# Expert outputs summed per token in DRAM by accumulating indirect transfers, in place of gathers at the end

## The chip, the core and the metric

The kernel runs as one program on one core of a Trainium2 chip. Its engines are TensorE (PE, whose weight loads are listed as PEld), VectorE (DVE), ScalarE (ACT) and GpSimd (POOL); SyncE (SP) issues most of the transfers, and POOL issues the indirect ones, whose rows are named by a list of indices in SBUF. The metric is the device time of one execution in microseconds; the time of a kernel is the median over its runs.

## The reference

The input x has 4 rows of 1024 tokens of 128 numbers. Two layers follow, each with two branches that read the same normalized x and are added to it:

```python
x = L0_attn_x
xn = _layernorm(x, axis=-1)
x = x + _L0_attn_ref(xn, ...) + _L0_ffn_ref(xn, ...)
xn = _layernorm(x, axis=-1)
x = x + _L1_attn_ref(xn, ...) + _L1_ffn_ref(xn, ...)
```

The first layer is an attention of 16 heads with one shared key and value head, and a SwitchHead attention: 8 heads with 8 experts each for values and outputs, of which gates choose two. The second is a FAVOR+ attention (16 heads, 64 random features; exponentials of queries and keys, sums over the tokens, no attention matrix) and a mixture of experts. The change is in the mixture:

```python
logits = xf @ gate_w + gate_b                    # 4096 tokens, 8 experts
top_w, top_i = jax.lax.top_k(logits, 2)
gw = jax.nn.softmax(top_w, axis=-1)
combine = (gw[:, :, None] * jax.nn.one_hot(top_i, E)).sum(axis=1)
for e in range(E):                               # 128 -> 512 -> 128
    h = jax.nn.gelu(xf @ w1[e] + b1[e], approximate=False)
    out = out + combine[:, e:e + 1] * (h @ w2[e] + b2[e])
shared = jax.nn.gelu(xf @ ws1 + bs1) @ ws2 + bs2
return (out + shared).reshape(orig_shape)
```

So only two of the eight experts count for a token, each with its share.

## The kernel before

**Layer 0** goes over the four rows b and, in each, over the heads; it lasts to about 3015 us of the span. TensorE's order of instructions is written out by hand; VectorE, ScalarE and POOL are ordered by the scheduler of the tile framework. In it, as soon as x of a row is whole, layer 1's normalization and its **router** run for that row (L222 to L280), scattered between heads of the next row. The router takes the two best experts per token (oh0, oh1), counts with two matmuls how many tokens of each expert came before, and so gives every (token, expert) pair a slot: expert e owns rows 4096e to 4096e + 4095 of the DRAM tensor `sorted_x`. `share` holds the two softmax weights. Then the row's normalized tokens are written there: for each of 8 tiles of 128 tokens VectorE makes `xslot` (L270, two buffers), and POOL issues two indirect scatters of it (L274), one per chosen expert. Each waits for the one before to land, as both write `sorted_x`. Before all that, behind row 0's first attention, `sorted_x` is filled with zeros by one SP transfer from a small zero tile (L535 to L542), since the last block of an expert is only partly used.

**Layer 1** has its order written by hand for TensorE and SP. Two things run in turn.

The attention of row b has two generators: `favor_keys` (19 steps) and `favor_queries` (20 steps). They run in five stages: keys of row 0; then queries of row 0 with keys of row 1; 1 with 2; 2 with 3; queries of row 3. These are 19, 39, 39, 39 and 20 steps. `project` (L957 to L969) starts each: qT or kT, and its square on POOL (L968), which `dg` (L1024) needs.

The filler is the rest of the mixture: `shared` (17 steps: the shared feed-forward) and then `experts` (L1288 on), 39 blocks of 256 rows with two half steps each, 78 half blocks. 39 is enough for every way in which the tokens can be divided over the experts; which expert a block has, and where it starts in `sorted_x`, is worked out by VectorE before (tile `block`, read by SP with value loads). A block j goes through `load` (SP: its rows xg from `sorted_x`, w1, w2; three buffers each), `turn` (two transposes on TensorE, L1306), `one` (8 matmuls pb, L1316, with gelu on ScalarE, L1322) and `two` (8 matmuls pe, L1331; a VectorE copy yb of the result, L1336; a store to the DRAM tensor `sorted_y`, L1337). Iteration j of the loop does load(j), turn(j-1), one(j-2), two(j-3), and gives way after `one` and after `two`.

The stages set how much filler goes beside each attention step, by a rate; with a rate of 1.0 in all stages the 95 filler steps are used up at the end of stage 2:

```python
for _ in run(*its):
    due += rate
    while due >= 1.0:
        due -= 1.0
        next(filler, None)
```

At the end `combine` (L1353 to L1367) fetches both expert rows of each token back: per tile of 128 tokens and per chosen expert one indirect gather on POOL from `sorted_y` (L1359; the row numbers are worked out from the slots, L940 to L953) and one VectorE multiply-add of it, by the share, into x (L1365). After four tiles SP writes the output's 256 KB (L1401). There are 64 gathers, 64 multiply-adds, 8 outputs; each gather waits for one of six y buffers.

Each engine works through its own queue in order, so an instruction that waits holds up all behind it there.

Of the kernel before, what the change touches and what calls it, by code (L numbers as in the profile page):

```python
# [9 lines left out]
F32 = mybir.dt.float32  # L10
I32 = mybir.dt.int32
BF16 = mybir.dt.bfloat16
AF = mybir.ActivationFunctionType
ALU = mybir.AluOpType
# [40 lines left out]
PER = SLOTS // MB  # L55

# [8 lines left out]
def two_layers(ctx: ExitStack, tc: tile.TileContext, a: dict, out: bass.AP):  # L65
# [84 lines left out]
    slot = fixed([P, 2, B, NT], "slot")  # L150
# [11 lines left out]
    sorted_x = hbm.tile([ME * SLOTS, D], F32, tag="sorted_x", name="sorted_x")  # L162
    sorted_y = hbm.tile([NBLK * MB, D], F32, tag="sorted_y", name="sorted_y")
# [58 lines left out]
    def router(b):  # L222
# [25 lines left out]
        for n in range(NT):  # L248
            nc.vector.tensor_tensor(mask[:, n, :], pcv[:, 0, n, :], filled, ALU.add)
            nc.vector.tensor_tensor(filled, pcv[:, 1, n, :], filled, ALU.add)  # L250
        for k, oh in enumerate((oh0, oh1)):
            to = rt.tile([P, NT, ME], F32, tag="to", name=f"to{b}_{k}")
            nc.vector.tensor_tensor(to, oh, mask, ALU.mult)
            nc.vector.tensor_reduce(slot[:, k, b, :], to, axis=AX.X, op=ALU.add)
        at_slot = rt.tile([P, 2, NT], I32, tag="at_slot", name=f"at_slot{b}")
        nc.vector.tensor_copy(at_slot, slot[:, :, b, :])
# [11 lines left out]
        for n in range(NT):  # L268
            xn = rt.tile([P, D], F32, tag="xslot", name=f"xslot{b}_{n}", bufs=2)
            nc.vector.tensor_scalar(  # L270
                xn, x[b][:, n, :], mv[:, n, 0:1], rstd[:, n : n + 1], ALU.subtract, ALU.mult
            )
            for k in range(2):
                nc.gpsimd.indirect_dma_start(  # L274
# [8 lines left out]
    with ExitStack() as l0:  # L283
# [219 lines left out]
        def mqa_out(b):  # L503
# [28 lines left out]
            if b == 0:  # L532
                nc.sync.dma_start(gw, a["gate_w"])
                nc.sync.dma_start(gb, a["gate_b"].unsqueeze(0).to_broadcast([P, ME]))
                empty = sw.tile([P, SE, P], F32, tag="gs", name="empty", bufs=3)  # L535
                nc.gpsimd.memset(empty, 0.0)
                flat = empty.rearrange("p e d -> p (e d)")
                n = ME * SLOTS * D // (P * SE * P)
                nc.sync.dma_start(
                    sorted_x.rearrange("(p n k) d -> p n (k d)", p=P, n=n),  # L540
                    flat.unsqueeze(1).to_broadcast([P, n, SE * P]),
# [355 lines left out]
    for e in range(1, ME):  # L897
# [4 lines left out]

    past = brief(0, NBLK, ME - 1, "past")
    full = [P, NBLK, ME - 1]
    nc.vector.tensor_tensor(
        past, bcast(num[:, 0:NBLK], ME - 1),
        upto[:, 0 : ME - 1].unsqueeze(1).to_broadcast(full), ALU.is_ge,
# [3 lines left out]
    nc.vector.tensor_tensor(  # L911
        past, past, nb[:, 0 : ME - 1].unsqueeze(1).to_broadcast(full), ALU.mult
    )
    nc.vector.tensor_reduce(of[:, 1, :], past, axis=AX.X, op=ALU.add)
    nc.vector.tensor_tensor(of[:, 1, :], num[:, 0:NBLK], of[:, 1, :], ALU.subtract)
    nc.vector.tensor_scalar(of[:, 1, :], of[:, 1, :], float(PER - 1), None, ALU.min)
    nc.vector.scalar_tensor_tensor(
        of[:, 1, :], of[:, 0, :], float(PER), of[:, 1, :], ALU.mult, ALU.add
    )
    block = fw.tile([P, 2, NBLK], I32, tag="block", name="block")  # L920
# [15 lines left out]

# [528 lines left out]
```

## Time and profile before

| | us |
|---|---|
| runs shown | 3592.8, 3598.83, 3599.55 |
| median | 3598.83 |
| profiled execution, its own time | 3601.22 |
| its span | 3599.4 |
| layer 1: stages 0 to 4 start at about | 3040, 3173, 3303, 3425, 3519 |
| last matmul ends at | 3568 |
| TensorE busy in the span | 3356.3 |

The mean granted clock of TensorE is 0.962 of full speed. In the profile a line such as `L1331 PE MATMUL pe<-w,hb` is a group of instructions: source line, engine, operation, what it writes and reads. "Busy" is the time in which an engine executes, "idle before" the time in which it stood still just before that instruction, with what ended that. Registers, semaphores and the issuing of transfers by SP are not counted as busy. In a table by stretches each engine has its busy time and, in brackets, its instructions; then come the granted clock, the share of time in which the 16 transfer engines were busy, and the rate.

### The profile page before, as it was taken

Reading aid. Unit: us, or ns where it says so; the run is one execution under the profiler, and the core shown is the slowest. Engines: PE = TensorE matmul, PEld = TensorE weight load, DVE = VectorE, ACT = ScalarE, POOL = GpSimd, SP = SyncE. Lnnn points to the kernel's source line nnn. Section 1 sums busy time; section 2 is a strip of 40 time slices with the busy share of each in tenths; the row PEclk is TensorE's granted clock in tenths of the full one; section 3 lists DMA queues with packets and bytes.
Section 4 is the critical chain, followed back from the end, with each engine's and each line's share of the span. In section 5 each row is a group of like instructions: output and inputs, shape, how many; then the busy total and the mean of one; then the engine's idle time right before and its main releaser. Section 6 shows DMA issues by size and latency. Waiting matters only on the chain.

```text
span 3599.4 us, 40579 instructions
## 1 busy us (share of the span) xinstructions
PE 3356.3 (93%) x14270; PEld 1682.1 (47%) x14270; DVE 2506.2 (70%) x4571; ACT 1613.6 (45%) x2800; POOL 1592.9 (44%) x2032
## 2 busy tenths in 40 slices
PE   6999999999999998999999989999999998999973
PEld 3444444444444443444444434444444443478852
DVE  6876678777777778777777687677777765355575
ACT  2344444444444443444445434444444454455521
POOL 3644445444454465444454554444644433100024
PEclk8999999999999998999999999999999998899976
DMA  3000000000410000000000000000000000024302
GB/s 84 19 14 14 21 14 28 7 19 12 180 50 19 12 20 20 19 12 19 14 23 12 17 23 12 19 19 14 27 15 13 6 1 14 31 76 140 104 19 55
DMA packets 146543, 111.46 MB, mean 31 GB/s; under 512 B 11482, under 2 KB 128740, under 8 KB 146340
## 3 DMA queue, kind: packets, MB, share of 16 engines
q1 hardware_dynamic: 142116, 100.46, 9.7%
q0 software_dynamic: 4096, 8.40, 0.8%
q8 instruction: 113, 1.85, 0.2%
q14 instruction: 90, 0.74, 0.1%
q10 hardware_dynamic: 128, 0.02, 0.0%
HBM read 77.12 MB, written 31.33 MB: 30 GB/s over the span
## 4 chain that ended last, share of the span: by engine, by line
PE 77%; DVE 14%; POOL 3%; issue 2%; DMA 2%; ACT 1%; SPq 1%; another core or an unknown queue 0%; POOLq 0%; DVEq 0%; ACTq 0%
PE cp L681 12%; PE ss L649 11%; PE po L702 11%; PE pv L632 11%; PE ov L460 6%; PE sT L470 5%; PE pTp L669 5%; PE mx L416 5%; DVE nmh L422 2%; DVE nms L654 2%; PE qks L613 1%; PE pb L1316 1%; PE pe L1331 1%; DMA sorted_x<-xslot,at_slot 1%; DVE mk L1051 1%
## 5 line engine op out<-in xcount | busy, mean ns | idle before, releaser
L422 DVE TENSOR_REDUCE nmh<-mx 128x1 f32<-128x512 f32 x1024 | 657.4, 680 | 353.6 <-PE mx L416 353.1
L621 POOL TENSOR_TENSOR g_o<-g_o 128x512 f32<-128x512 f32 x256 | 324.9, 1269 | 1224.4 <-DVE g_o L706 1002.4
L477 ACT ACTIVATE pT<-sT 128x512 f32<-128x512 f32 x1024 | 556.3, 601 | 408.0 <-PE sT L470 403.9
L632 PE MATMUL pv<-vw,xnT 128*128 128x512 f32 x1024 | 486.9, 609 | 18.3 <-DVE nmh L422 9.1
L681 PE MATMUL cp<-pTs,vs 128*128 128x512 f32 x1024 | 463.2, 606 | 39.6 <-DVE pTs L673 32.4
L649 PE MATMUL ss<-xnT,qTs 128*128 128x512 f32 x1024 | 492.2, 602 | 6.7 <-DVE gv L636 3.8
L702 PE MATMUL po<-ow,cTs 128*128 128x512 f32 x1024 | 471.8, 593 | 2.5 <-ACT ps L652 2.5
L652 ACT COPY ps<-ss 128x512 f32<-128x512 f32 x512 | 298.6, 587 | 351.7 <-PE ss L649 332.0
L654 DVE TENSOR_REDUCE nms<-ps 128x1 f32<-128x1024 f32 x256 | 310.6, 1213 | 188.7 <-ACT ps L652 188.1
L656 ACT ACTIVATE ps<-ps,nms 128x1024 f32<-128x1024 f32 x256 | 294.2, 1149 | 180.4 <-DVE nms L654 179.4
L636 DVE TENSOR_TENSOR gv<-pv,gates 128x512 f32<-128x512 f32 x512 | 334.7, 681 | 32.2 <-POOL x L712 12.4
L621 POOL TENSOR_TENSOR gv<-gv 128x512 f32<-128x512 f32 x256 | 328.6, 1284 | 34.4 <-DVE gv L636 34.1
L706 DVE TENSOR_TENSOR g_o<-po,go 128x512 f32<-128x512 f32 x512 | 328.4, 680 | 19.1 <-PE po L702 14.2
L681 PEld LDWEIGHTS cp<-pTs,vs 128*128 128x128 f32 x1024 | 193.9, 193 | 287.5 <-issue 231.7
L416 PE MATMUL mx<-ks,qs 72*128 72x512 bf16 x1024 | 310.0, 380 | 11.8 <-DVE nmh L422 5.2
L470 PE MATMUL sT<-qs,ks 75*128 75x512 bf16 x1024 | 308.2, 382 | 11.4 <-DVE ob L499 3.7
L632 PEld LDWEIGHTS pv<-vw,xnT 128*128 128x128 f32 x1024 | 196.0, 194 | 243.8 <-issue 153.9
L649 PEld LDWEIGHTS ss<-xnT,qTs 128*128 128x128 f32 x1024 | 190.9, 191 | 195.4 <-issue 122.7
L669 PE MATMUL pTp<-ident,ps 128*128 128x128 f32 x2048 | 270.1, 275 | 11.6 <-ACT ps L656 9.1
L669 PEld LDWEIGHTS pTp<-ident,ps 128*128 128x128 f32 x2048 | 239.8, 141 | 81.9 <-issue 20.4
L702 PEld LDWEIGHTS po<-ow,cTs 128*128 128x128 f32 x1024 | 179.6, 190 | 157.5 <-issue 136.4
L460 PE MATMUL ov<-pT,va 128*32 128x512 f32 x2048 | 248.5, 601 | 0.0
(269 smaller groups left out, 3901.2 us busy)
## 6 DMA issues: line engine op xcount, KB each, us to landing
w<-in_w_dram SPq DMA_DIRECT2D x78, 256.0 KB
vw<-in_v_w_dram SPq DMA_DIRECT2D x32, 512.0 KB
ow<-in_o_w_dram SPq DMA_DIRECT2D x32, 512.0 KB
sorted_x<-empty SPq DMA_DIRECT2D x1, 16384.0 KB
qs<-qd SPq DMA_DIRECT2D x144, 64.0 KB
xg<-sorted_x SPq DMA_DIRECT2D x39, 128.0 KB
sorted_y<-yb SPq DMA_DIRECT2D x39, 128.0 KB
qd<-qp SPq DMA_DIRECT2D x12, 256.0 KB
```

The source lines that it names most:

```text
L416: nc.tensor.matmul(sc, lhsT=qs[0:NPAIR, i, ts(n, P)], rhs=ks[0:NPAIR, ts(kc, 512)], start=True, stop=True,)
L422: nc.vector.tensor_reduce(halves[:, i, n, kc : kc + 1], sc, axis=AX.X, op=ALU.max)
L460: nc.tensor.matmul(ov[32 * i : 32 * i + 32, :], lhsT=va[:, kt, :], rhs=pT, start=(kt == 0), stop=(kt == NT - 1),)
L470: nc.tensor.matmul(sc, lhsT=ks[:, ts(kt, P)], rhs=qs[:, i, ts(c, 512)], start=True, stop=True,)
L477: nc.scalar.activation(pT, sc, AF.Exp)
L621: nc.gpsimd.tensor_tensor(g[:, 0:4, :], g[:, 0:4, :], g[:, 4:8, :], ALU.add)
L632: nc.tensor.matmul(pv, lhsT=xnT[b][:, ts(n, P)], rhs=unit[u, "w"][0][:, ts(c, 512)], start=True, stop=True,)
L649: nc.tensor.matmul(sc, lhsT=qT[:, ts(n, P)], rhs=xnT[b][:, ts(c, 512)], start=True, stop=True)
L654: nc.vector.tensor_reduce(nm, p, axis=AX.X, op=ALU.max, negate=True)
L669: nc.tensor.transpose(pt[:, ts(k, P)], p[:, ts(4 * k4 + k, P)], ident)
L681: nc.tensor.matmul(cp, lhsT=v[:, kt, :], rhs=pT[:, kt, :], start=(kt == 0), stop=(kt == NT - 1),)
L702: nc.tensor.matmul(po, lhsT=cT[:, ts(qt, P)], rhs=unit[u, "w"][1][:, ts(c, 512)], start=True, stop=True,)
```

## The change

The gathers go, and each block adds its weighted rows to its tokens' sums itself.

- A row of `sorted_x` gets two more numbers (ROW = 130): the token's number, as 32-bit integer, and its share. The router makes one `xslot` per scatter (16 instead of 8 per row of x, still two buffers), and POOL writes the two columns with small copies.
- Rows of `sorted_x` that no token fills hold "nobody": zeros, and the token number 4096, which is a row of the sums that nobody reads. 256 such rows are put behind the last expert, and blocks past the end of the work read these.
- Two DRAM tensors `sums[0]`, `sums[1]` (4224 x 128 each) are filled with zeros ahead of `sorted_x`. The fill of `sorted_x` is by rows of 520 bytes.
- `two` multiplies each half of its result by the share column of xg (two VectorE instructions in place of one copy) and POOL adds it to `sums[q]` at the rows that xg's token column names, by an indirect transfer that accumulates. `sorted_y` and its store go, so do the row numbers. xg has four buffers, and is held until those transfers have read its indices.
- At the end SP reads each chunk of 512 tokens of both sums (16 reads of 256 KB, into the three buffers of w1), VectorE adds them to x (16 adds of 128x512), SP writes the 8 outputs.
- The rates become 0.84, 0.45, 0.45, 0.45, 1.2, so that half blocks go beside the steps of all stages; the few left follow stage 4.
- The squares of L968 move from POOL to VectorE; the zeros of va1 are written once instead of per row.

```diff
+ROW = D + 2
...
+    sorted_x = hbm.tile([ME * SLOTS + MB, ROW], F32, tag="sorted_x", name="sorted_x")
+    sums = [hbm.tile([B * T + P, D], F32, tag=f"sum{q}", name=f"sum{q}") for q in range(2)]
+    token = const.tile([P, B * NT + 1], I32, tag="token", name="token")
+    nc.gpsimd.iota(token, pattern=[[P, B * NT + 1]], base=0, channel_multiplier=1)
...
         for n in range(NT):
-            xn = rt.tile([P, D], F32, tag="xslot", name=f"xslot{b}_{n}", bufs=2)
-            nc.vector.tensor_scalar(
-                xn, x[b][:, n, :], mv[:, n, 0:1], rstd[:, n : n + 1], ALU.subtract, ALU.mult
-            )
             for k in range(2):
+                xn = rt.tile([P, ROW], F32, tag="xslot", name=f"xslot{b}_{n}_{k}", bufs=2)
+                nc.vector.tensor_scalar(
+                    xn[:, 0:D], x[b][:, n, :], mv[:, n, 0:1], rstd[:, n : n + 1],
+                    ALU.subtract, ALU.mult,
+                )
+                i = b * NT + n
+                nc.gpsimd.tensor_copy(xn[:, D : D + 1].bitcast(I32), token[:, i : i + 1])
+                nc.gpsimd.tensor_copy(xn[:, D + 1 : ROW], share[:, k, b, n : n + 1])
                 nc.gpsimd.indirect_dma_start(
...
-                n = ME * SLOTS * D // (P * SE * P)
+                for to in sums:
+                    n = B * NT + 1
+                    nc.sync.dma_start(
+                        to.rearrange("(n p) d -> p n d", p=P),
+                        empty[:, 0:D].unsqueeze(1).to_broadcast([P, n, D]),
+                    )
+                full = sw.tile([P, SE, P], F32, tag="gs", name="nobody", bufs=3)
...
+                n = (ME * SLOTS + MB) // P
                 nc.sync.dma_start(
-                    sorted_x.rearrange("(p n k) d -> p n (k d)", p=P, n=n),
-                    flat.unsqueeze(1).to_broadcast([P, n, SE * P]),
+                    sorted_x.rearrange("(n p) d -> p n d", p=P),
+                    nobody.unsqueeze(1).to_broadcast([P, n, ROW]),
                 )
...
-    rows = fw.tile([P, NS], I32, tag="rows", name="rows")
-    nc.vector.tensor_copy(rows, row)
...
-        nc.gpsimd.tensor_tensor(sq, dT, dT, ALU.mult)
+        nc.vector.tensor_tensor(sq, dT, dT, ALU.mult)
...
+    va = late([P, NT, 2, 4, 32], "va1")
+    nc.gpsimd.memset(va, 0.0)
...
-            xg = ff.tile([P, MB // P, D], F32, tag="xg", name=f"xg{j}", bufs=3)
+            xg = ff.tile([P, MB // P, ROW], F32, tag="xg", name=f"xg{j}", bufs=4)
...
             yb = ff.tile([P, MB // P, D], F32, tag="yb", name=f"yb{j}")
-            nc.vector.tensor_copy(yb.rearrange("p q d -> p (q d)"), py[:, 0:MB])
-            nc.sync.dma_start(
-                sorted_y[ts(j, MB), :].rearrange("(q p) d -> p q d", p=P), yb
-            )
+            for q in range(MB // P):
+                nc.vector.tensor_scalar(
+                    yb[:, q, :], py[:, ts(q, D)], xg[:, q, D + 1 : ROW], None, ALU.mult
+                )
+                nc.gpsimd.indirect_dma_start(
+                    out=sums[q][:, :],
+                    out_offset=bass.IndirectOffsetOnAxis(
+                        ap=xg[:, q, D : D + 1].bitcast(I32), axis=0
+                    ),
+                    in_=yb[:, q, :], in_offset=None, compute_op=ALU.add,
+                )
...
-        ((0,), 1.0), ((0, 1), 1.0), ((1, 2), 1.0), ((2, 3), 1.0), ((3,), 1.0),
+        ((0,), 0.84), ((0, 1), 0.45), ((1, 2), 0.45), ((2, 3), 0.45), ((3,), 1.2),
...
     for b in range(B):
-        for n in range(NT):
-            combine(b, n)
...
+        for q in range(T // TC):
+            xs = x[b][:, ts(q, 4), :]
+            for to in sums:
+                y = ff.tile([P, MH], F32, tag="w1", name=f"y{b}_{q}", bufs=3)
+                y = y.rearrange("p (n d) -> p n d", d=D)
+                rows = to[ds(b * T + q * TC, TC), :]
+                nc.sync.dma_start(y, rows.rearrange("(n p) d -> p n d", p=P))
+                nc.vector.tensor_tensor(xs, xs, y, ALU.add)
+            nc.sync.dma_start(out[b, ts(q, TC), :].rearrange("(n p) d -> p n d", p=P), xs)
```

## The prediction

> **What bounds the kernel now.** I read the page's totals and 40 slices first, then the busy time of each engine in stretches that I cut at the stages of layer 1, then the groups, waits and timeline inside them. Totals, slices and granted clock:
>
> ```profile
> PE 3356.3 (93%) x14270; PEld 1682.1 (47%) x14270; DVE 2506.2 (70%) x4571; ACT 1613.6 (45%) x2800; POOL 1592.9 (44%) x2032
> PE   6999999999999998999999989999999998999973
> PEclk8999999999999998999999999999999998899976
> ```
>
> TensorE is the bound nearly everywhere; only the last two slices fall. The stretches (PE, PEld, DVE, ACT, POOL busy, then clock, DMA share, GB/s): the first loads, the old fill of sorted_x, stages 0 to 4 of layer 1, and the tail after the last matmul:
>
> ```profile
> 24.00:32.00 8.00, 7.53 (x20) 3.86 (x20) 2.89 (x11) 2.46 (x3) 0.35 (x2) 1.00 1.21 290
> 955.00:991.00 36.00, 34.70 (x145) 15.96 (x143) 29.51 (x59) 21.51 (x38) 13.04 (x17) 1.00 1.02 421
> 3040.00:3171.00 131.00, 118.64 (x549) 64.27 (x548) 56.03 (x145) 49.08 (x62) 22.96 (x25) 0.87 0.10 32
> 3171.00:3303.00 132.00, 124.05 (x1018) 105.42 (x1018) 77.97 (x167) 75.51 (x117) 6.37 (x6) 0.97 0.41 118
> 3303.00:3425.00 122.00, 117.63 (x958) 101.03 (x957) 73.63 (x160) 69.22 (x106) 6.36 (x6) 0.96 0.38 108
> 3425.00:3519.00 94.00, 64.90 (x458) 45.16 (x458) 63.82 (x140) 21.15 (x19) 26.06 (x26) 0.71 0.08 22
> 3519.00:3568.00 49.00, 30.41 (x208) 22.37 (x208) 38.98 (x92) 13.40 (x14) 22.14 (x24) 0.78 0.18 47
> 3568.00:3599.40 31.40, 0.00 (x0) 0.00 (x0) 7.71 (x22) 0.00 (x0) 17.75 (x19) 0.50 0.25 67
> ```
>
> Stages 1 and 2 are full of TensorE work (94 and 96%), because one half block goes into every attention step; stages 3 and 4 have none left and are 69 and 62% full, at 0.71 and 0.78 clock. What ends waits there (3430 to 3575), and what a half block costs (groups of stage 2):
>
> ```profile
> PE dg L1024 <- POOL ksq L968: 11.9, 1, 11.9
> PE qt L1133 <- ACT qE L989: 10.8, 4, 5.8
> PE oT1p L1187 <- DVE o L1177: 8.3, 2, 6.9
> ```
> ```profile
> L1331 PE MATMUL pe<-w,hb 128*128 128x128 f32 x304 | 39.2, 285 | 0.0
> L1316 PE MATMUL pb<-xgT,w 128*128 128x256 f32 x139 | 33.0, 380 | 0.1
> ```
>
> The square on POOL is late by 11.9 us since gathers, each waiting for a VectorE add, stand ahead of it in POOL's queue. The indirect transfers, as their lines list them (scatter, gather), and the last of the tail's timeline:
>
> ```profile
> L274 POOL DMA_INDIRECT sorted_x<-xslot,at_slot x64: 960/985/1307, 1016.8 to 3100.4; - x64
> L1359 POOL DMA_INDIRECT y<-sorted_y,rows x64: 942/947/1237, 3425.9 to 3592.9; - x64
> 1019.60 0.96 POOL L274 DMA_INDIRECT sorted_x<-xslot,at_slot  x1 [1.54 <-DMA sorted_x<-xslot,at_slot]
> 3592.93 0.95 POOL L1359 DMA_INDIRECT y<-sorted_y,rows  x1 [0.31 <-issue]
> 3595.91 0.37 SPq L1401 DMA_DIRECT2D out_dram<-x  x1
> ```
>
> A scatter takes 0.96 us to issue, and the next waits 1.54 us for its landing; the tail is gathers every 1.25 us, then one output.
>
> **The change part by part.** The profiled execution took 3601.2 us (span 3599.4 and 1.8 around it), 2.4 above the median of 3598.8. I sum against 3601.2 and subtract 2.4.
>
> *Stage 0.* 19 steps at rate 0.84 give 15 filler steps instead of 19: two shared steps (5.2 us each, 10.4) and two half blocks (2.1 each, with waits 5) leave. POOL's squares and the slot bookkeeping that held VectorE's cTs, for which TensorE sat 7.3 us, leave too. -20; ends -12 (the idle stays) and -23.
>
> *Stages 1 to 4.* Half blocks cost (39.2 + 33.0 + 6.5 for the transposes) over 37, 2.1 us, 2.08 at full clock. A stage's own matmuls are 117.6 - 78.7 = 39 in stage 2 and 64.9 x 0.71 / 0.97 = 47 in stage 3: 43; stage 4 has 30.4 x 0.78 / 0.97 = 25. Together 3 x 43 + 25 + 78 x 2.08 + 10.4 = 326 us of TensorE work, against 397 us (3171 to 3568) now. Spread out, a stage has 80 us of TensorE beside some 69 of VectorE (57 its own, 9 blocks at about 1.1, 2.45 squares); in order on both, I take 91% full, between stage 1's 94 and less: 359 us, -38. Ends: 96%, 340 (-57); 85%, as if VectorE's waits of stage 3 stayed in part, 383 (-14). Half blocks left for after stage 4 (3 by the rates) are in the 326.
>
> *Squares to VectorE.* 8 x 1.89 us leave POOL; the nearest row, a 128x1024 multiply, has a median of 1.225 us (to 2.29). Counted in the 69; the 11.9 of waiting is gone in the 359. What is late next is qE and o, on ACT and VectorE.
>
> *Weighting and accumulates.* Each block's 0.42 us copy becomes two multiplies of 0.35 (a 128x128 tensor_scalar: 0.346), and its store on SP becomes two POOL issues, 78 in all. No accumulating transfer is in the trace. The issue I take as the scatter's 0.96, the landing as its 1.54; below they cannot go (more work than a scatter of the same rows), above I allow twice the issue and 5 us of landing. POOL has under 7 of 122 us in stage 2, so the issues lie beside other work. But xg now holds shares and indices, so block k's load into one of four buffers waits on SP for block k-4's accumulates, and behind it wait the next weights, then the transposes on TensorE. Loop: multiplies 0.7, two issues 2, landing 1.6 to 3, SP's load 0.4 and landing 2: 7 to 9, take 8. An iteration (two half blocks) has 9.9 us in stages 1 to 3 (87 us, 8.8 blocks): hidden, 0 (to +13). In stage 4, at 1.2 half blocks a step, it has 6.3 (25 + 24 x 2.08 us of TensorE over 12 blocks): 12 x 1.7 = 20, less some 6 that buffered blocks cover: +14 (+5 to +35).
>
> *Gone from stages 3, 4 and the tail.* 64 gathers and 64 adds (20.9 us of VectorE); already in the 359 and below.
>
> *Tail.* Now 31.4 us after the last matmul. After: the last accumulates land (4.5 to 5 us), then eight chunks in SP's order: two reads into three shared buffers, two 128x512 adds, an output. Each chunk's output waits for its adds, and the next reads stand behind it: 0.37 + 2 x 0.45 issue + about 2 landing (a 256-KB output: 1.94) + two adds, one beside the second read, about 0.65 to 0.7 on the path and small gaps: 4.75 x 8 = 38, and 2 for the last output: 45. +13.5 (+7 if reads overlap, +20).
>
> *Fill.* Instead of 16.8 MB at 421 GB/s in 4-KB pieces, SP issues two zero fills (8448 rows of 512 B, 4.3 MB) and 33024 rows of 520 B, 17.2 MB. The nearest row for small pieces is the load of x and weights at 24 to 32 us, 512-B packets at 290 GB/s. So 15 us, then 41 (at 421) to 59 (at 290), and 100 as the far bound for pieces that are not the row's: from 953 to between 1009 and 1068, by the nearest row 1027. POOL reaches row 0's first scatter at about 1030 (1017 now, plus the work ahead of it in the new order), known to some 10 us, and layer 0's gate sums stand behind it in its queue: +6 (0 to +38). The loads of weights queued behind on SP land in time as long as the fill ends before about 1070.
>
> The Trainium skill, "DMA: Bandwidth & Descriptors", section "How a descriptor splits into AXI transactions", says that a piece which does not start on a 256-B boundary pays for the bytes ahead of it. Rows of 520 B start at multiples of 8; averaged, some 20.5 beats against 16 for an aligned 512-B row. By it the 59 us would be an estimated 76 and the fill would end at 1044, +14 instead of +6; the trace has no unaligned rows, so no run here shows it yet.
>
> *Scatters.* A tile per transfer instead of per token block, two buffers as before: VectorE's 0.35 multiply is doubled (8 more a row) and each must wait for the scatter two before; two tiny POOL copies (about 0.1) go ahead of each scatter. VectorE waits 32.0 us for scatters now, 8 per row; 8 more waits of up to 2 us per row, of which TensorE feels a part since it loses 5 to 7 us per row there now: +3 for each of rows 0 to 2, +9 (0 to +24).
>
> *At nothing:* the va memsets (3 x 1.81 on POOL, idle there), 39 stores fewer on SP, clamps of the block numbers (hidden under stage 0's matmuls; about 0.5 if bare).
>
> Sum: -20 - 38 + 14 + 13.5 + 6 + 9 = -15.5: 3585.7, less 2.4, **3583**.
>
> The Trainium skill, "SBUF — State Buffer" (the trap of VectorE blocking POOL's DMAs), says that VectorE's two-port copies keep POOL from writing descriptors. The gathers' 942 to 1237 ns beside VectorE's adds show no such stall. Were each issue 3 us by that rule, the loop would be an estimated 12 us, as in rival B.
>
> **The rivals.**
> A, slower: the fill is late. POOL waits for it at the first scatter and layer 0's sums wait behind. Small rows speak for it, the 290 GB/s against. It decides once the stall is over 22 us (fill later than about 1052, under 205 GB/s for the rows); at 45 us of stall 3622.
> B, slower: accumulates are slow. At 11.5 us a loop, stage 4's 12 blocks cost another 42: 3625; stages 1 to 3, at 1.6 a block, up to as much again. It decides from a loop of about 9.3 us.
> C, faster: stages reach stage 2's 96% (340, -19) and the loop stays hidden (-14): 3550. Against it: VectorE and ACT chains that stage 3 shows.
> D, nothing gained: 88% (371, +12) and a serial tail of 20 instead of 13.5 eat the gain: 3601, within a hair of before.
>
> **How the numbers follow.** Forecast 0.45, A 0.16, B 0.16, C 0.12, D 0.11. 0.2% is 7.2 us, about what a measurement of this kernel can tell. Faster: 0.45 + 0.12 = 0.57; within 0.11; slower 0.32. The likeliest case's own range is 3560 to 3592. The whole range goes from C with a hidden tail, 3538, into A and B, 3634.
>
> **What will show it.** Stage 0 starts near 3055; it and the others last some 111, 94, 87, 87 and, with the drain, 104 us; last matmul near 3538; PE waits on xg in stage 4 only; no wait for squares; a tail of 44 to 45 us paced by SP. The fill's end and POOL's first scatter show A; the gap from an accumulate's issue to the next xg issue shows B. The forecast is wrong if spread-out half blocks push VectorE or ACT onto TensorE's path, or the reads of the tail overlap.

## The result and the profile after

The changed kernel is slower: 3640.47 us median against 3599.19 us, a ratio of 1.0122 (95% interval 1.009 to 1.0154). 3583 had been forecast; the measured time also lies above the upper end of the range, 3634. The profiled execution took 3654.58 us (span 3652.5); a second profile of the same kernel on another chip, e0 below, has a span of 3653.1 where the kernel before had its median at 3602.89 (ratio 1.014). I read the two as one. The profiled execution is the slowest of its four (the others took 3637 to 3641 us), so what is read from it adds up to 68 us over the forecast, the median to 57.

The span divides at three marks: the end of layer 0, taken as how late the softmax maxima of its last scores come against the kernel before (the 256 VectorE reductions nms paired in order); the first projection of keys; and the last matmul. In us:

| | before | after | after, again (e0) | forecast change | measured change |
|---|---|---|---|---|---|
| layer 0 late by | 0 | 55.4 | 56.3 | +15 | +55 |
| stage 0 | 133.8 | 122.1 | 121.1 | -20 | -12 |
| stages 1 to 4 with drain | 393.9 | 380.6 | 382.7 | -24 | -13 |
| tail after the last matmul | 31.5 | 53.5 | 53.0 | +13.5 | +22 |

The signs are as forecast, every term is worse than its central value, and 40 of the 68 us between forecast and measurement lie in layer 0. The transfer rates there (the DMA view of 952 to 1060 us, 40 slices; the kernel after, and what ended POOL's and TensorE's longest waits, with POOL's first scatter):

```profile
GB/s 0 93 290 289 282 291 280 293 283 272 241 168 172 164 176 165 171 168 173 179 214 252 268 272 271 272 184 164 163 163 168 165 169 162 165 203 252 229 209 263
1058.23 1.31 POOL L284 DMA_INDIRECT sorted_x<-xslot,at_slot  x1 [23.50 <-DMA sorted_x<-nobody]
1061.47 0.35 DVE L277 TENSOR_SCALAR xslot<-x,mv,rstd 128x128 f32<-128x128 f32 x1 [24.95 <-DMA sorted_x<-xslot,at_slot]
PE pv L654 <- DVE nmh L432: 24.3, 1, 24.3
```

The zero fills of the sums, in aligned 512-byte rows, go at 290 GB/s. The 520-byte rows begin at about 971 us, go at 270 to 290 at first, at 162 to 179 in two stretches of some 25 us, and faster again between and after those. Next to nothing else moves meanwhile, as the DMA views of one faster and one slower stretch show (1008 to 1020 and 1024 to 1046 us; 3.11 MB in 5990 packets are 520 bytes each):

```profile
DMA packets 5992, 3.14 MB, mean 262 GB/s; under 512 B 0, under 2 KB 5990, under 8 KB 5990
DMA packets 6975, 3.63 MB, mean 165 GB/s; under 512 B 0, under 2 KB 6975, under 8 KB 6975
```

The 33024 rows take 86 us (200 GB/s on average; 93 us and 184 GB/s in e0), and the rate falls and rises in the same parts of the fill in all seven profiles with such rows. So the fill ends at about 1058 us, 23.5 us after POOL came to its first scatter (30.9 in e0). VectorE's third xslot waits for a buffer of that scatter for 24.95 us, the reduction nmh stands behind it in VectorE's queue, and TensorE stands 24.3 us for nmh.

Groups that tell of the scatters (before: VectorE waited 32.0 us in 19 waits, POOL 17.1 in 6; of the 90.9 us of VectorE now, 24.95 are the wait behind the fill) and of the accumulates:

```profile
  DMA sorted_x<-xslot,at_slot: 90.9, 48
  DVE xslot L277: 53.3, 28
L1341 POOL DMA_INDIRECT sum<-yb,xg x78: 1540/1548/2277, 3242.3 to 3604.2; - x78
DMA to landing us min/median/max: 3.2/3.3/4.0
SPq L1295 <- DMA sum<-yb,xg: 151.1, 34, 8.4
PE xgT L1305 <- DMA xg<-sorted_x: 25.0, 13, 4.2
```

An accumulate takes 1.55 us to issue and lands 3.3 us after its issue began (a scatter: 0.99 and 2.3). SP stands 151 us for accumulates before the loads of xg; TensorE feels 25.0 us of it at the transposes, directly. Each of the 35 loads of xg from the fifth on was issued 3.4 to 5.3 us (median 3.5) after the issue of the accumulate that frees its buffer, so at about its landing. The stretches of the kernel after, stages 0 to 3, stage 4 with the drain, and the tail (columns as in the prediction), and SP's issues at the start of the tail:

```profile
3096.00:3218.00 122.00, 112.58 (x536) 58.92 (x536) 61.40 (x155) 42.95 (x52) 23.12 (x52) 0.88 0.12 32
3218.00:3312.00 94.00, 86.11 (x687) 69.00 (x690) 66.71 (x144) 58.70 (x74) 22.70 (x17) 0.87 0.28 58
3312.00:3414.00 102.00, 91.19 (x724) 73.07 (x720) 71.11 (x155) 57.71 (x73) 28.99 (x21) 0.88 0.33 70
3414.00:3508.00 94.00, 84.98 (x718) 69.52 (x710) 70.77 (x153) 54.23 (x68) 27.51 (x19) 0.93 0.34 69
3508.00:3599.00 91.00, 74.08 (x540) 63.98 (x536) 45.92 (x102) 44.17 (x74) 39.78 (x27) 0.96 0.51 107
3599.00:3652.50 53.50, 0.00 (x0) 0.00 (x0) 11.69 (x18) 0.00 (x0) 5.52 (x4) 0.55 0.47 123
```
```profile
3605.49 2.99 SPq L1395 DMA_DIRECT2D y<-sum  x2
3611.59 0.38 SPq L1397 DMA_DIRECT2D out_dram<-x  x1
3612.07 1.05 SPq L1395 DMA_DIRECT2D y<-sum  x2
3616.87 0.38 SPq L1397 DMA_DIRECT2D out_dram<-x  x1
3617.30 1.10 SPq L1395 DMA_DIRECT2D y<-sum  x2
```

The stages are evenly 81 to 92% full now. The tail's first read is issued 6.5 us after the last matmul, when the last accumulate into `sums[0]` (issued at 3602.31, the last but one of all) has landed; then each chunk takes 5.3 us.

### The profile page after: what moved, and what is told of

It reads as the page before. It is cut to its first block, busy times and chain, and to the rows that moved or that the text cites. A ratio compares the mean times of both kernels' runs of the same rounds, so it can differ in the third digit from the quotient of the medians.

```text
span 3652.5 us, 40876 instructions
## 1 busy us (share of the span) xinstructions
PE 3366.1 (92%) x14270; PEld 1682.9 (46%) x14270; DVE 2526.2 (69%) x4597; ACT 1643.4 (45%) x2823; POOL 1653.5 (45%) x2166
## 4 chain that ended last, share of the span: by engine, by line
PE 75%; DVE 13%; DMA 5%; POOL 3%; issue 2%; ACT 1%; another core or an unknown queue 1%; SPq 1%; DVEq 0%; POOLq 0%; ACTq 0%
PE cp L703 12%; PE ss L671 11%; PE po L724 10%; PE pv L654 10%; PE ov L470 6%; PE sT L480 5%; PE pTp L691 5%; PE mx L426 5%; DMA sorted_x<-xslot,at_slot 2%; DVE nmh L432 2%; DVE nms L676 2%; PE pb L1315 1%; PE qks L635 1%; PE pe L1331 1%; DMA sum<-yb,xg 1%
## 5 line engine op out<-in xcount | busy, mean ns | idle before, releaser
L691 PEld LDWEIGHTS pTp<-ident,ps 128*128 128x128 f32 x2048 | 240.2, 142 | 88.7 <-issue 25.3
```

The source lines that it names most:

```text
L691: nc.tensor.transpose(pt[:, ts(k, P)], p[:, ts(4 * k4 + k, P)], ident)
```

## The experiments

Where a run was timed, its ratio to the kernel before on the same chip is given. Three kernels were timed on two chips each, and their ratios differ by up to 0.2%; the changed kernel itself was not timed on the chip of e1 to e4. So the parts are read from the profiles. Each row is one profiled execution, in us:

| run | layer 0 late by | first keys to last matmul | tail | span | ratio (95%) |
|---|---|---|---|---|---|
| before | 0 | 527.7 | 31.5 | 3599.4 | 1 |
| after, again (e0) | 56.3 | 503.8 | 53.0 | 3653.1 | 1.0140 (1.0121 to 1.0159) |
| e1 wide fill | 26.4 | 503.4 | 51.1 | 3621.1 | 1.0077 (1.0052 to 1.0102) |
| e2 xslot on POOL | 79.5 | 494.0 | 53.1 | 3668.7 | 1.0210 (1.0193 to 1.0227) |
| e3 outputs on ScalarE | 58.1 | 496.8 | 38.3 | 3633.9 | 1.0134 (1.0113 to 1.0156) |
| e4 six xg buffers | 56.3 | 469.4 | 53.3 | 3618.9 | 1.0074 (1.0055 to 1.0093) |
| e7 no adding | 53.7 | 478.5 | 50.1 | 3621.6 | one execution |
| e12 rates 1.0 | 51.4 | 580.4 | 5.5 | 3676.7 | 1.0254 (1.0231 to 1.0276) |
| e9 wide fill, copies on VectorE | 16.9 | 504.3 | 52.0 | 3614.2 | one execution |
| e10 wide fill, three xslot buffers | 17.0 | 496.1 | 54.5 | 3608.3 | one execution |
| e8 = e1 + e3 + e4 | 26.4 | 477.9 | 37.2 | 3581.5 | 0.9913 (0.9896 to 0.9931) |
| e14 = e8 again | 24.4 | 463.5 | 36.4 | 3563.7 | 0.9924 (0.9908 to 0.9941) |
| e5 = e8, squares on POOL | 25.4 | 475.8 | 37.1 | 3577.7 | 0.9962 (0.9950 to 0.9973) |
| e15 = e5 again | 25.3 | 478.7 | 37.9 | 3581.9 | 0.9958 (0.9942 to 0.9973) |
| e6 = e8, rates 1.0 | 26.8 | 497.8 | 5.6 | 3570.9 | 0.9945 (0.9926 to 0.9965) |
| e11 = e8 + cures of e9, e10 | 11.1 | 463.9 | 37.2 | 3552.4 | 0.9914 (0.9894 to 0.9935) |
| e13 = e11, blocks end with stage 3 | 15.5 | 463.0 | 14.6 | 3532.5 | 0.9858 (0.9841 to 0.9875) |

From the first keys to the last matmul, e0, e4, e7, e8 and e14 (length, then TensorE's busy time first and the granted clock third from the end):

```profile
3096.30:3600.10 503.80, 447.50 (x3183) 332.54 (x3183) 315.43 (x707) 258.36 (x339) 142.07 (x134) 0.91 0.31 65
3096.20:3565.60 469.40, 435.78 (x3184) 323.88 (x3183) 314.22 (x707) 258.18 (x339) 142.37 (x134) 0.93 0.32 70
3093.00:3571.50 478.50, 435.90 (x3184) 328.03 (x3183) 315.13 (x707) 256.98 (x339) 98.38 (x134) 0.92 0.24 69
3066.40:3544.30 477.90, 445.67 (x3183) 331.02 (x3183) 314.62 (x707) 257.96 (x339) 141.93 (x134) 0.90 0.32 69
3063.80:3527.30 463.50, 432.23 (x3184) 323.26 (x3183) 314.51 (x707) 256.94 (x339) 142.32 (x134) 0.93 0.33 71
```

e8 and e14 are one kernel, and this stretch differs by 14 us. TensorE is busy 445.7 and 432.2 us with the same matmuls, at a granted clock of 0.90 and 0.93, and stands still for 32.2 and 31.3 us. So in a single profile the busy time of these stages can move by 13 us with the clock, while the time that TensorE stands still is the steadier witness. The tail repeats within 4 us where its code is the same, layer 0's lateness within 5 us with the wide fill and within 7 us with the fill by rows.

**e0, the changed kernel again.**

> The changed kernel itself once more, so that the others can be compared with it on one chip. If the first profile (3652.5, late by 55 us at the end of layer 0, last matmul 31 us later than before, a tail of 53.5) is typical, this one shows the same within 10 us and the ratio to the kernel before is 1.010 to 1.017. Rival: the wait for the fill varies by chance; then its gap in row 0 is far from 25 to 34 us here.

The gap in row 0 was 32 us, against 25 in the first profile, so the wait for the fill does vary by some 7 us; the rest agrees, and the ratio is within what was expected.

**e1, the fill in wide pieces.** Six rows of nobody side by side in the tile; their dummy tokens still run through 128 values down the rows (4096 to 4223, one for each row of a tile, in the changed kernel too, and not 4096 alone).

```diff
-                nobody = full.rearrange("p e d -> p (e d)")[:, 0:ROW]
+                nobody = full.rearrange("p e d -> p (e d)")[:, 0 : 6 * ROW]
...
-                    sorted_x.rearrange("(n p) d -> p n d", p=P),
-                    nobody.unsqueeze(1).to_broadcast([P, n, ROW]),
+                    sorted_x.rearrange("(n p k) d -> p n (k d)", p=P, n=n),
+                    nobody.unsqueeze(1).to_broadcast([P, n, 6 * ROW]),
```

> The changed kernel with sorted_x filled in pieces of six rows (3120 bytes) instead of one row (520 bytes); the same bytes land, the rows of nobody still have dummy tokens that differ within a block. Theory 'small rows': the fill ran at 163 to 171 GB/s because of its 520-byte pieces, so with 3120 bytes it goes at 350 GB/s or more and ends before 1025 us; POOL's wait of 23.5 us for the fill and TensorE's gap of 24.3 us go, layer 0 ends some 25 us earlier, and the median falls from 3640 to about 3615. Rival 'unaligned rows': pieces that start off a 256-byte boundary are slow whatever their length; then the fill stays near 170 to 200 GB/s, ends near 1050, and the median stays at 3635 to 3645.

The same stretch of 952 to 1060 us, of e1:

```profile
GB/s 256 290 281 290 290 318 409 406 396 386 392 392 399 396 403 398 391 394 393 388 401 355 314 29 0 0 0 0 0 25 25 0 34 25 28 25 29 189 25 0
```

The fill goes at 386 to 409 GB/s and is done at about 1013 us, POOL does not wait for it at its first scatter, TensorE's gap is gone and layer 0 is late by 26.4 instead of 56.3 us. So writing row by row was the cost.

Which property of the rows it was is not shown. Pieces of 3120 bytes also start off 256-byte boundaries (at multiples of 16 instead of 8), so such a start alone does not make a piece slow; rows of 520 bytes went at 262 GB/s in one part of the fill and at 165 in another, so neither does the length alone. The wide pieces are longer, fewer and start elsewhere all at once, and no run has 512-byte rows off a boundary or padded rows on one. The Trainium skill, "DMA: Bandwidth & Descriptors", section "How a descriptor splits into AXI transactions", has the right sign, since the rows off the boundary are dearer on average than the aligned ones. Its words are of bytes that are fetched, so using it for writes was the prediction's step. By its beats some 230 GB/s would follow as an estimate (290 times 16 over 20.5 beats, times 520 over 512 bytes); 200 were measured on average, 184 in e0, with stretches of 165.

**e2, xslot on POOL.**

```diff
-                nc.vector.tensor_scalar(
+                nc.gpsimd.tensor_scalar(
                     xn[:, 0:D], x[b][:, n, :], mv[:, n, 0:1], ...
```

> The changed kernel with the 64 xslot multiplies on POOL instead of VectorE, so that VectorE waits for no scatter. Theory 'VectorE held by two buffers': of layer 0's 55 us of lateness, the 6 to 11 us in each of the rows come from VectorE's 90.9 us of waits at xslot (32.0 before the change), and the 24.3 us gap too, since it was VectorE that stood still behind POOL's wait for the fill; then at least 20 us go, up to 45, and the median is 3595 to 3620. Rival 'POOL's queue': what is late are layer 0's gate sums that stand behind scatters on POOL; they get 16 x 0.45 us more per row ahead of them, and the median rises to 3645 to 3665.

The theory fell: VectorE no longer waits for any scatter, and layer 0 is late by 79.5 us, 23 more. The 24 us gap stays, at another place: TensorE's waits of 1030 to 1130 us in e2 are

```profile
PE sT L480 <- DVE gv L658: 24.2, 1, 24.2
PE ss L671 <- DVE gv L658: 12.1, 1, 12.1
PE mx L426 <- DVE nmh L432: 10.4, 1, 10.4
```

gv waits for buffers that POOL's gate sums have to empty, and those stand behind the scatters. Making an xslot on POOL took 0.79 us, not 0.45, so 12.7 us a row came into POOL's queue:

```profile
L277 POOL TENSOR_SCALAR xslot<-x,mv,rstd x64: 787/793/1140, 963.2 to 3177.8; 128x128 f32<-128x128 f32 x64
```

What counts in the stretch of scatters is the time that POOL's queue needs; VectorE's waits are one way in which that reaches TensorE.

**e9 and e10, two cures of the scatters, each on top of the wide fill.** e9 has both tiny copies as `nc.vector.tensor_copy`; e10 has three xslot buffers:

```diff
-                nc.gpsimd.tensor_copy(xn[:, D : D + 1].bitcast(I32), token[:, i : i + 1])
-                nc.gpsimd.tensor_copy(xn[:, D + 1 : ROW], share[:, k, b, n : n + 1])
+                nc.vector.tensor_copy(xn[:, D : D + 1].bitcast(I32), token[:, i : i + 1])
+                nc.vector.tensor_copy(xn[:, D + 1 : ROW], share[:, k, b, n : n + 1])
...
-                xn = rt.tile([P, ROW], F32, tag="xslot", name=f"xslot{b}_{n}_{k}", bufs=2)
+                xn = rt.tile([P, ROW], F32, tag="xslot", name=f"xslot{b}_{n}_{k}", bufs=3)
```

> The wide fill, and the 128 tiny copies of token and share on VectorE instead of POOL. Theory 'POOL's work in the scatter stretch': 16 x 0.32 us leave POOL's queue in each row, and layer 0's lateness (26 us with the wide fill, 7 to 10 in each of rows 0 to 2) falls by 3 to 5 us a row, to 11 to 17. Rival 'two buffers': VectorE still waits for the scatter two before, POOL waits longer for VectorE, and the lateness stays at 24 to 30.

> The wide fill, and three xslot buffers instead of two (more do not fit). Theory 'two buffers': POOL's 53.3 us of waits for xslot and VectorE's 90.9 for the scatters mostly go, and the lateness at the end of layer 0 falls from 26 us to 8 to 16. Rival 'POOL's work': each scatter still waits for the landing of the one before and the copies stay, so the lateness stays at 20 to 28.

Each takes 9.4 us off layer 0's lateness (26.4 to 16.9 and 17.0). For e9 that is the least that was expected; for e10 it lies between the theory (8 to 16) and the rival (20 to 28). In e10 POOL's waits for xslot fell to 32.9 us in 18, from 48.2 in 28 in e1. Both together, in e11, leave 11.1 us:

> The kernel with wide fill, outputs on ScalarE and six xg buffers, and both cures of the scatters: three xslot buffers, and the copies of token and share on VectorE. With the wide fill alone layer 0 was late by 26.4 us against the kernel before, with three buffers 17.0, with the copies on VectorE 16.9. If the two are separate causes, 8 us are left and the median is 3550 to 3560; if both remove the same wait, 16 are left and it is 3560 to 3570.

That lies between the two expectations, but e13, whose layer 0 is the same, is late by 15.5 us, where one shared wait was expected. So they are at least partly the same wait; how much is left open. The median of 3558.71 is where separate causes were expected, but on a chip on which the kernel before was 10 us faster than on e8's, so it decides nothing.

**e4, six xg buffers** (`bufs=4` becomes `bufs=6`).

> The changed kernel with six xg buffers instead of four. Theory 'loop through the accumulates': SP's waits of 151 us for accumulates before xg loads go, and with them TensorE's 25.0 us of waits at the transposes; the stages get 15 to 20 us shorter in all, median about 3622. Rival 'three weight buffers': SP stands just as long for w1 and w2 (it waits 80.7 us for pe there now), and TensorE's waits move behind other loads; 0 to -6 us.

First keys to last matmul 469.4 instead of 503.8 us: 34 us, twice what was expected. By the lines above, TensorE stands still for 33.6 instead of 56.3 us, 23 less, close to the 25.0 that the profile put down to xg; the other 12 us are the same matmuls taking 435.8 instead of 447.5 us, at a higher granted clock. This gap holds in all profiles with the rates of the change and the squares on VectorE: TensorE stands still for 47 to 56 us in the seven with four buffers and writes that add, and for 31 to 34 us in the four with six. Whether the clock came with the buffers or by chance is not shown. TensorE no longer waits for xg, and SP waits for something else, as the rival said, without harm (e4, SP's waits from 3218 us):

```profile
SPq L1299 <- PE pe L1331: 185.1, 29, 16.5
SPq L1297 <- PE pb L1315: 62.4, 1, 62.4
```

By stages: stages 3 and 4 with the drain take 162.9 to 164.5 us together in all kernels with six buffers, the rates of the change and squares on VectorE, 184 to 190 in those with four.

**e7, plain writes in place of accumulates** (`compute_op=ALU.add` left out).

> The changed kernel with plain indirect writes in place of the accumulating ones; the adding is left out, so a token's sum holds only the expert written last. An accumulate takes 1.55 us to issue and lands 3.3 us after, a scatter 0.97 and 2.3. Theory 'price of accumulating in the loop': the loop from a block's last matmul to the next rows is about 1.6 us shorter, and where four buffers let it pace the stages (the waits of 25 us for xg, the 33 us that six buffers gained) 12 to 25 us go between the last keys' projection and the last matmul; the tail is about 2 us shorter too. Rival 'it is not the transfer's price but where SP stands': the stages change by less than 6 us.

From the first keys to the last matmul 25 us less than e0: 5 in stage 0, which holds no accumulates, 8 in stages 1 and 2, 12 in stages 3 and 4, with the tail 3 us shorter. In the stretch for which numbers had been given, from the last keys' projection, it is 187.2 to 174.8, the least that was expected.

```profile
L1341 POOL DMA_INDIRECT sum<-yb,xg x78: 952/957/1691, 3231.3 to 3574.6; - x78
DMA to landing us min/median/max: 2.2/2.3/4.1
PE xgT L1305 <- DMA xg<-sorted_x: 14.4, 11, 2.9
```

Of the 25 us, 12 are again matmuls at a higher clock, those of stage 0 among them. TensorE stands still for 42.6 us, against 56.3 in e0 and 33.6 in e4. So of the 23 us of standing still that four buffers cost, about 14 are the price of adding rather than writing, by this one execution; the rest is the loop itself.

**e3, outputs issued by ScalarE** (`nc.sync.dma_start(out...)` becomes `nc.scalar.dma_start(out...)`).

> The changed kernel with the 8 output transfers issued by ScalarE instead of SP, so that the next reads of the sums do not stand behind an output that waits for VectorE. Theory 'serial tail': a chunk takes 5.3 us because its reads are issued only after the output before; with that gone the three buffers and two issues of 0.5 us pace it, 2.5 to 3 us a chunk, the tail after the last matmul falls from 53.5 to 32 to 36 us and the median to about 3620. Rival 'the transfers themselves': reads and outputs share the transfer engines and take as long when they overlap; the tail stays above 48 us.

All sixteen reads go out in one run of 24 us (e3, SP's timeline), and the tail is 38.3 us instead of 53; a little less was gained than forecast:

```profile
3602.10 23.95 SPq L1395 DMA_DIRECT2D y<-sum  x16
```

The timed ratio, 1.0134, can't be told from e0's 1.0140 on another chip, so a gain in time is not shown by e3 alone; that the 15 us are there in the tail is shown by the profile. In e8 the three cures together gave 72 us of span and, timed beside e0 on one chip, 80 us (3653.02 to 3573.19).

**e8, the three together.**

> The changed kernel with three of the causes taken away together: the fill in pieces of six rows, outputs issued by ScalarE, six xg buffers. Theory 'four separate places': the gains add, 25 to 30 (fill) + 15 (tail) + 20 to 28 (loop) off some 3645, so 3570 to 3585, faster than before by 0.3 to 0.8%, with the scatters' 26 us still in layer 0. Rival 'one bound behind the other': what one of them saves is given back to another wait, and the time stays above 3600.

The gains add: 0.9913, faster than both kernels. The layer-0 lateness of e1, the tail of e3 and the stages of e4 appear side by side.

**e6 and e12, the rates at 1.0 again,** in e8 and in the changed kernel.

```diff
-        ((0,), 0.84), ((0, 1), 0.45), ((1, 2), 0.45), ((2, 3), 0.45), ((3,), 1.2),
+        ((0,), 1.0), ((0, 1), 1.0), ((1, 2), 1.0), ((2, 3), 1.0), ((3,), 1.0),
```

> The kernel with wide fill, outputs on ScalarE and six xg buffers, with all five rates at 1.0 again, so that half blocks are used up at the end of stage 2. Theory 'spreading is worth what the empty stages were': stages 1 and 2 go back to about 130 and 122 us, stages 3 and 4 have nothing but the attention and take about 75 and 40; from the first keys to the last matmul 490 to 505 us instead of 478, so the median is 12 to 27 us over 3573. Rival 'the gathers' waits were the loss': without gathers stages 3 and 4 take 60 and 30 and the spreading brings nothing, 3565 to 3578.

> The changed kernel with the rates at 1.0 again and nothing else undone. Theory 'spreading moves the sums to the very end': the matmuls end later than in the changed kernel, since an iteration of 6.5 us meets a loop of 8 to 9 us through four buffers, by 5 to 45 us; but the tail of 53 us shrinks to 6 to 10; together 3615 to 3655, against 3640 to 3653 of the changed kernel. Rival 'spreading pays for itself': the loop paces stages 1 to 3 so much that more than 50 us are lost there, and it is over 3660.

Without spreading the matmuls of e6 end 20 us later (497.8 instead of 477.9), near the middle of what was expected. But its tail is 5.6 us, not 37: all blocks are done at the end of stage 2, and SP's reads lie beside stages 3 and 4. SP's timeline of e6 shows them as one group:

```profile
3449.19 111.72 SPq L1401 DMA_DIRECT2D y<-sum  x16
```

That is about even: 20 us of stages against e8, 34 against its repetition e14, for 31 us of tail, and the span of e6 lies between those of the two. The timed medians don't decide it either: 3573.91 and 3573.19, with ratios of 0.9945 and 0.9913 (0.9924 in e14) on different chips. In the changed kernel the rival was right: e12 is 1.0254. Stages 1 and 2 take 164 and 162 us there, 8.6 for each of their 38 iterations, against 130 and 115 us, 6.4 each, in e6 with six buffers. So the loop through four buffers paces e12, and TensorE's waits for xg more than double:

```profile
PE xgT L1305 <- DMA xg<-sorted_x: 57.7, 21, 6.0
```

So spreading pays in the change since it hides the accumulates' loop; where six buffers do that, it gives back at the tail what it saves in the stages.

**e13, the blocks finished with stage 3.** All cures, and rates 0.84, 0.66, 0.66, 0.66, 1.2.

> All cures together (wide fill, outputs on ScalarE, six xg buffers, three xslot buffers, token and share copies on VectorE) and rates 0.84, 0.66, 0.66, 0.66, 1.2, by which the blocks end with stage 3. Theory 'the sums must be whole before the last attention': stages 1 to 3 take 316 us together (297 us of TensorE work at 94%), stage 4 about 43 without half blocks, the reads and adds of the tail lie beside stage 4, and some 6 us come after the last matmul: 12 to 20 us below the same kernel with the changed kernel's rates, 3530 to 3548. Rival 'one tail for another': the reads hold up stage 4's adds into x and the output is no earlier; 3550 to 3565.

0.9858: the fastest here, 53.8 us below the kernel before on that chip, and 25 us below e14, which was timed beside it, at a median of 3540.96 (some of the 25 is the scatters' cure). Beside e11, which differs in the rates alone and was timed on another chip (0.9914), the stretch to the last matmul is the same, 463.0 and 463.9 us, and the tail is 14.6 instead of 37.2. The stretches of e13, stages 1 to 4 and the tail:

```profile
3167.60:3270.00 102.40, 95.42 (x810) 79.06 (x810) 71.57 (x159) 62.68 (x88) 35.76 (x25) 0.98 0.42 89
3270.00:3375.00 105.00, 99.76 (x823) 85.47 (x822) 75.12 (x167) 61.98 (x87) 41.89 (x29) 0.92 0.46 98
3375.00:3475.00 100.00, 93.67 (x788) 79.53 (x787) 72.83 (x163) 59.21 (x83) 39.49 (x26) 0.97 0.45 93
3475.00:3518.00 43.00, 31.57 (x236) 23.70 (x234) 37.75 (x76) 16.35 (x19) 8.09 (x6) 0.88 0.39 90
3518.00:3532.50 14.50, 0.00 (x0) 0.00 (x0) 5.35 (x8) 0.00 (x0) 0.00 (x0) 0.61 0.67 196
```

Stages 1 to 3 are 93 to 95% full, stage 4 takes 43 us, and 22 of the 37 us of tail lie beside it. The tail of 14.5 us is more than the 6 expected, as the last blocks ran into stage 4 and the first read was issued at 3489.75:

```profile
3489.75 34.88 SPq L1401 DMA_DIRECT2D y<-sum  x16
```

**e5, e14 and e15, the squares on POOL again in e8.**

> The kernel with wide fill, outputs on ScalarE and six xg buffers, with the eight squares on POOL again. Theory 'POOL is free now': nothing waits in POOL's queue for VectorE for long, VectorE loses 8 x 1.2 us of work, and the time is the same as or up to 8 us below 3573. Rival 'squares stand behind accumulates': each waits for yb on VectorE, TensorE's dg matmuls wait up to 5 us in each stage, and the time is 5 to 20 us above.

> The kernel with wide fill, outputs on ScalarE and six xg buffers, squares on VectorE, once more, beside the next one on the same chip: 0.990 to 0.996 of the kernel before.

> The same with the squares on POOL. If squares behind accumulates in POOL's queue cost time, 5 to 18 us over the run beside it; if the move of the squares is worth nothing either way, as the two profiles say (475.8 and 477.9 us from the first keys to the last matmul), within 5 us of it.

On one chip, with six executions of each: 3565.96 with the squares on VectorE, 3578.55 on POOL, ratios 0.9924 and 0.9958. Their move is worth 12.6 us, as the rival of e5 said, though POOL waits for no gathers any more. The two earlier profiles hid it by their clocks (e8 0.90, e5 0.91, while e14 had 0.93). From the first keys to the last matmul TensorE stands still for 38.9 and 41.3 us with the squares on POOL (e5, e15), 32.2 and 31.3 with them on VectorE (e8, e14), so 7 to 10 of the 12.6 us are waits. Where they lie is partly shown: in e15 TensorE waits 10.2 us for va before kv, in e14 1.0, and va comes after the squares through dg and mk; the squares themselves stood behind accumulates that wait for yb (POOL idle 14.4 us in 2 waits). The lines are e5's and e15's stretches and e15's waits.

```profile
3064.80:3540.60 475.80, 436.93 (x3183) 330.46 (x3182) 307.10 (x699) 256.88 (x339) 156.51 (x142) 0.91 0.32 69
3065.40:3544.10 478.70, 437.42 (x3183) 327.34 (x3182) 307.35 (x699) 257.63 (x339) 157.10 (x142) 0.91 0.32 69
PE kv L1087 <- DVE va L1077: 10.2, 3, 5.2
  DVE yb L1343: 14.4, 2
```

## Why the prediction was wrong

It was wrong by the sum of terms that had all been named, most of them near the far end of their bounds at once. What failed were mostly sizes, first of all those of the fill and the scatters, which hold 40 of the 68 us, and one overlap, that of the accumulates' loop in stages 1 to 3. By its steps:

- **Fill, +6 taken, +25 to +32 measured.** This is the step that failed first. The nearest row, 290 GB/s, was for aligned 512-byte packets, and the sum went by it; the rows of 520 bytes went at 162 to 179 for half of the fill, 200 on average. They took 86 us, 93 in e0, not 59: nearer to the far bound of 100, which had been written down beside the sum and not taken into it. Rival A's condition, a fill later than 1052, came true; its price of 45 us was for a longer stall than the 23.5 to 31 us of POOL. (The estimate of 76 us by beats counts the 8 bytes more of a row twice; it comes to 75. It was nearer than 59, and still short.)
- **Scatters, +9 taken, +24 measured** (6.2, 9.1 and 9.2 in rows 0 to 2, e0): the upper bound. VectorE waited 59 us more for scatters, but 25 of them are the wait behind the fill; the other 34 are 8.5 a row, half of what 8 waits of up to 2 us would give. TensorE felt nearly all of that, about 8 a row, where I had taken 3. POOL's queue was lengthened at the same time by the copies and by its own waits for xslot; e2, e9 and e10 show that POOL's queue counts.
- **Stage 0, -20 taken, -12 measured.** The scatters of row 3 lie in it, but that they are the reason is not shown: with their cures it takes 112.7 to 118.4 us, without them 116 to 122 (111 in e2), and part of that moves with the clock (0.88 to 0.92).
- **Stages 1 to 4, -38.** Right, and a little small: with six buffers, where the loop is hidden, they take 348 us in e4, -46; full to 93%, not 91. In the changed kernel itself the forecast with the loop, 373 us, was missed by 8 to 10, and that by some luck: TensorE stood still for 45 to 47 us, about as many as the forecast's 47 (33 for stages that are not full and 14 for the loop), but the shares were 24 and 21 to 23. The rest is TensorE's work, 336 us instead of 326, at a granted clock of 0.88 to 0.94 where the sum had taken some 0.97. Why the clock was lower is not shown.
- **Loop, +14 taken, 23 measured** as TensorE standing still (e0 against e4), 34 with the clock, at the end of the bound. The loop itself was sized rightly: the issue was 1.55 us and not 0.96, the landing 3.3 after the issue began and not 2.5, and e12, which it paces, shows 8.6 us an iteration, where 8 had been taken. What failed is the step that called it hidden in stages 1 to 3 because an average iteration has 9.9 us. In stages 1 and 2 it cost some 10 us (195.5 in e0, 185.2 in e4). Iterations are uneven: in these three stages the results of successive blocks come 4.4 to 20.5 us apart. Rival B's mechanism is what happened, below its price. Of the Trainium skill's rule on VectorE's two-port copies ("SBUF — State Buffer") there was no sign that decides: no issue took 3 us, 75 of 78 took 1.54 to 1.68, and the two longest, 2.28, lie beside VectorE's 128x1024 squares; most of the copies beside the others read TensorE's results and not SBUF, so the rule was hardly put to the test.
- **Tail, +13.5 taken, +22 measured,** above its bound of +20. SP's order was read rightly. A chunk took 5.3 us instead of 4.75 (of which the terms that were named give 3.9 to 4.0, the rest being called small gaps), and the last accumulates 6.5 instead of 4.5 to 5.
- **Squares.** Counted in, and their sign was right (e14, e15).
- **The range.** Fill, scatters and loop had bounds that lean to one side and were added at values near the low ends, and rivals A and B were priced one at a time. The upper ends of fill, scatters, loop and tail together give +75 on the forecast; what was measured is 69 above its 3585.7 in the profiled execution, 57 above 3583 in the median.

## What to carry to other kernels

When a row grows by a few numbers, look at every transfer that writes such rows: 520 bytes instead of 512 took the fill from 290 to 200 GB/s on average, with stretches at 165, and bundling six rows gave 390. When a store becomes an accumulate whose list of indices lives in the input buffer, the input buffer is held through the issue and the landing, so give it more buffers before counting what the change brings (here six instead of four took away 23 us in which TensorE stood still). And when all results go into one sum, finish its writers before the last independent work, since reading it back is serial and nothing is left to hide it: the same reads cost 53 us after the last matmul, 37 with outputs on another queue, and 6 to 15 beside attention work.

## What the runs showed of the hardware that was not expected

- Accumulating indirect transfers of 128 rows of 512 bytes: 1.55 us of POOL to issue and 3.3 to land, against 0.96 and 2.3 for plain indirect writes of the same rows (e7, which also shows what the difference is worth in the loop).
- Writes of 520-byte rows, with next to nothing beside them: 162 to 179 GB/s in two stretches of the fill in the first profile and 136 to 169 in e0's, 200 to 290 in others, in the same parts of the fill each time; 512-byte rows go at 290 and 3120-byte pieces at 386 to 409. What sets fast rows apart from slow ones is not shown.
- One instruction that subtracts a per-partition number from 128x128 numbers and multiplies by another takes 0.79 us on POOL (e2) and 0.35 on VectorE.
- One kernel's stages took 14 us more or less from profile to profile with nearly the same standing still, since the same matmuls took 445.7 us at a granted clock of 0.90 and 432.2 at 0.93 (e8, e14).
